# A two-layer vision block on one core: evacuations, norm statistics and the order of the stages changed

## The chip, the cores and the metric

The kernel runs on one core of a Trainium2 chip. The metric is the device time of one execution in microseconds (us). The core has five engines with a program each: TensorE (PE; its weight loads are shown apart as PEld), VectorE (DVE), ScalarE (ACT), GpSimd (POOL) and SyncE (SP), which here only issues DMAs. They meet through semaphores. Matrix products go to PSUM[...].

## The reference

The input is 32 images of 56 x 56 tokens with 96 channels, float32. Two layers follow each other; each adds a mixer and a feed-forward network to the running value:

```python
x = x + attention(_ln_c(x))          # 7x7 windows, shifted by 3, 3 heads of 32, relative bias
t = t + ffn0(_ln_t(t))               # 96 -> 384 -> 96, operands rounded to fp8 (5,2), sums to (5,10)
x = x + ssm(_ln_c(x))                # norm again, expand to 2x192, gate, scan along the width, 192 -> 96
t = t + ffn1(_ln_t(t))

def _ln_c(v, eps=1e-6):
    m = jnp.mean(v, axis=-1, keepdims=True)
    s = jnp.var(v, axis=-1, keepdims=True)
    return (v - m) / jnp.sqrt(s + eps)
```

So there are four norms over the 96 channels of a token, called here "a" (attention), "f" (first network), "e" (state-space mixer, which the code folds into one norm) and "g" (second network). The scan of the mixer is written as a product with a 56 x 56 triangular matrix for each of 192 channels.

## The kernel before

The work is cut in 128 blocks of 14 image rows, held as a tile `xb` of 112 partitions (two window rows of 56 columns) by 7 x 96 values: 7 rows of tokens in each partition. Ten such tiles are in use in turn. A block is loaded, runs through all stages over several steps of the loop, is summed up in place and is stored from the same tile.

A norm has two stages. The first takes mean and variance of each of the 7 tokens of a partition, and GpSimd makes the power of -1/2; the second applies them:

```python
def ln_stats(i, name, scale, shift):
    xb = xtiles[i]
    st = one.tile([TP, G, 6], F32, tag=f"st_{name}", ...)
    mv = two.tile([TP, G, 2], F32, tag=f"mv_{name}", ...)
    for g in range(G):                                   # G = 7
        nc.vector.bn_stats(st[:, g, :], xb[:, g, :])
        nc.vector.bn_aggr(mv[:, g, :], st[:, g, :])
    rs = two.tile([TP, G], F32, tag=f"rs_{name}", ...)
    nc.vector.tensor_scalar(rs, mv[:, :, 1], scale, shift, op0=ALU.mult, op1=ALU.add)
    nc.gpsimd.tensor_tensor(rs, rs, neg_half, ALU.pow)
    state[name, i] = mv, rs

def ln_norm(i, name, dtype):
    ...
    for g in range(G):
        nc.vector.tensor_scalar(xn[:, g, :], xb[:, g, :], mv[:, g, 0:1], rs[:, g : g + 1],
                                op0=ALU.subtract, op1=ALU.mult, ...)
```

The products use PSUM tiles of two banks, four of them in turn. An output projection writes 4 tokens' columns to the first bank and 3 to the second, and each part is added to `xb` right after its own products:

```python
def out_banks(name):
    po = banks(name)                                     # [128, 2, 512], one of four
    ...                                                  # parts: (0, 4, bank 0), (4, 7, bank 1)

def att_out(i):                                          # tile "pr" in the profile
    xb = xtiles[i]
    for g0, g1, po in out_banks(f"pr_{i}"):
        for g in range(g0, g1):
            matmul(po[:, g - g0, :], ot[:, g]..., wo)
        add_to(xb, g0, g1, po)                           # VectorE

def ffn_out(i, layer):                                   # tiles "py_f", "py_g"
    for g0, g1, po in out_banks(f"py_{nm}"):
        for g in range(g0, g1):
            for hc in range(3):
                matmul(po[:, g - g0, :], hq[:, hc, ...], w2q[:, hc, :], ...)
        nc.scalar.copy(y16[:, g0:g1], po)
    nc.vector.tensor_tensor(y16, y16, b2q..., ALU.add)
    nc.gpsimd.tensor_tensor(xb, xb, y16, ALU.add)
```

`matmul` and `transpose` chain TensorE's instructions, so that they keep the order in which the stages are called; the other engines' instructions are put in an order by the framework. The loop calls the stages of different blocks in each step `t`; `run(lag, ...)` works on block `t - lag`, and `scan_some()` does one of the six scan units that each group of four blocks gives:

```python
for t in range(nblocks + 8):
    load(t + 2)
    run(0, att_tokens)              # tr_a
    run(7, ffn_tokens, 1)           # tr_g
    run(2, mix_tokens)              # tr_e
    run(0, att_qk)                  # qk
    run(7, ffn_hidden, 1)           # ph_g
    scan_some()
    run(1, ln_norm, "f", F8)
    run(0, att_v)                   # pv
    run(2, mix_expand, 0, 4)        # pu
    run(0, att_scores)              # sab, sc
    run(-1, ln_stats, "a", 1.0, LNC_EPS)
    run(7, ffn_out, 1)              # py_g
    run(7, store)
    run(2, mix_expand, 4, 7)        # pu
    if ...: scans += [...]          # every fourth step: six units
    run(1, ffn_tokens, 0)           # tr_f
    scan_some()
    run(6, mix_turn, 0, 4)          # gt
    run(0, att_values, nkeys)       # av
    scan_some()
    run(1, ffn_hidden, 0)           # ph_f
    run(6, mix_turn, 4, 7)          # gt
    scan_some()
    run(6, mix_out, 0)              # so
    run(0, att_back)                # tr_o
    run(6, mix_out, 1)              # so
    run(6, ln_stats, "g", 1.0, LNT_EPS)
    run(-1, ln_norm, "a", F32)
    scan_some()
    run(1, ffn_out, 0)              # py_f
    run(1, stats_e)
    run(0, att_out)                 # pr
    run(6, ln_norm, "g", F8)
    run(0, ln_stats, "f", 1.0, LNT_EPS)
    run(1, ln_norm, "e", F32)
    scan_some()
```

Of the kernel before, what the change touches and what calls it, by code (L numbers as in the profile page):

```python
# [23 lines left out]
C = 96  # L24
# [11 lines left out]
TP = 2 * HW  # L36
G = 7
# [6 lines left out]
HALF = NPAIR * W2  # L44
MASKED = -1.0e30
LNC_EPS = 1e-6
LNT_EPS = 1e-5
# [7 lines left out]
def kernel(  # L55
# [27 lines left out]
    nc = tc.nc  # L83
    nimg = x.shape[0]
    nblocks = nimg * NBLK
# [3 lines left out]
    one = ctx.enter_context(tc.tile_pool(name="one", bufs=1))  # L89
    two = ctx.enter_context(tc.tile_pool(name="two", bufs=2))  # L90
# [6 lines left out]
    def queued(ins):  # L97

        if last[0] is not None:
            tc.add_manual_dep(ins.ins, last[0], order, reason="order of the stages")  # L100
        last[0] = ins.ins.name

    def matmul(*args, start=True, stop=True):
        queued(nc.tensor.matmul(*args, start=start, stop=stop))  # L104
# [4 lines left out]
    def banks(name):  # L109

        return psum.tile([128, 2, 512], F32, tag="ps", name=name)
# [14 lines left out]
    xtiles = {}  # L126

    def load(i):
        if i >= nblocks:
            return  # L130
        xb = xpool.tile([TP, G, C], F32, tag="xb", name=f"xb_{i}")
        for dst, src in block_dmas(i, x, xb):
            nc.sync.dma_start(dst, src)
        xtiles[i] = xb
# [73 lines left out]
    wso = weights([2, C], F32, "wso")  # L208
# [85 lines left out]
    for w in range(HW):  # L294
        eng = nc.scalar if w % 2 else nc.sync
# [44 lines left out]
    xws, vs, gTs, xqs = [], [], [], []  # L340
    for n in range(2):
# [4 lines left out]
        gT = const.tile([128, 4 - n, 2, TP], F32, name=f"gT_{n}")  # L346
# [19 lines left out]

    def ln_stats(i, name, scale, shift):

        xb = xtiles[i]
        st = one.tile([TP, G, 6], F32, tag=f"st_{name}", name=f"st_{name}{i}")  # L370
        mv = two.tile([TP, G, 2], F32, tag=f"mv_{name}", name=f"mv_{name}{i}")
        for g in range(G):
            nc.vector.bn_stats(st[:, g, :], xb[:, g, :])  # L373
            nc.vector.bn_aggr(mv[:, g, :], st[:, g, :])
        rs = two.tile([TP, G], F32, tag=f"rs_{name}", name=f"rs_{name}{i}")
        nc.vector.tensor_scalar(rs, mv[:, :, 1], scale, shift, op0=ALU.mult, op1=ALU.add)
        nc.gpsimd.tensor_tensor(rs, rs, neg_half, ALU.pow)  # L377
        state[name, i] = mv, rs

    def ln_norm(i, name, dtype):  # L380
        xb = xtiles[i]
        mv, rs = state.pop((name, i))
        saturate = {"saturate": False} if dtype == F8 else {}
        xn = one.tile([TP, G, C], dtype, tag=f"xn_{name}", name=f"xn_{name}{i}")
        for g in range(G):
            nc.vector.tensor_scalar(  # L386
                xn[:, g, :],
                xb[:, g, :],
                mv[:, g, 0:1],
                rs[:, g : g + 1],  # L390
                op0=ALU.subtract,
                op1=ALU.mult,
                **saturate,
            )
        state["n" + name, i] = xn

# [13 lines left out]
    def out_banks(name):  # L410

        po = banks(name)
        parts = []
        for n, (g0, g1) in enumerate(((0, 4), (4, 7))):
            parts.append((g0, g1, po[0:TP, n, 0 : (g1 - g0) * C].rearrange("p (g c) -> p g c", c=C)))
        return parts

    def add_to(xb, g0, g1, po):
        nc.vector.tensor_tensor(xb[:, g0:g1, :], po, xb[:, g0:g1, :], ALU.add)  # L419

    state = {}
# [8 lines left out]
    def att_qk(i):  # L430
        xw = xws[i % 2]
        for n, dst in ((0, qT), (1, kT)):
            pq = banks(f"qk_{i}_{n}")
            for half in range(2):
                matmul(
                    pq[0:C, half, 0:HALF],
                    wqkv[:, n * C : (n + 1) * C],
                    xw[:, half * HALF : (half + 1) * HALF],
                )
            dst2 = dst[:, 0:NTOK].rearrange("c (h t) -> c h t", h=2)  # L440
            if n == 0:
                nc.scalar.copy(dst2, pq[0:C, :, 0:HALF])
            else:
                nc.vector.tensor_copy(dst2, pq[0:C, :, 0:HALF])

    def att_v(i):
        xw = xws[i % 2]
# [124 lines left out]
    def ffn_out(i, layer):  # L572
        w2q, b2q = ffns[layer][2:4]
        xb = xtiles[i]
        hq = state.pop(("hq", layer, i))
        nm = f"{'fg'[layer]}{i}"
        y16 = one.tile([TP, G, C], F16, tag="y16", name=f"y16_{nm}")
        for g0, g1, po in out_banks(f"py_{nm}"):
            for g in range(g0, g1):
                for hc in range(3):  # L580
                    matmul(
                        po[:, g - g0, :],
                        hq[:, hc, g * TP : (g + 1) * TP],
                        w2q[:, hc, :],
                        start=(hc == 0),
                        stop=(hc == 2),
                    )
            nc.scalar.copy(y16[:, g0:g1], po)  # L588
        nc.vector.tensor_tensor(y16, y16, b2q[:, None, :].to_broadcast([TP, G, C]), ALU.add)
        nc.gpsimd.tensor_tensor(xb, xb, y16, ALU.add)  # L590
# [65 lines left out]
            pt[0:C].rearrange("c b (s w) -> c (b s) w", w=RS)[:, 0 : 4 * n, 0:HW],  # L656
        )

    def mix_out(i, part):
        if part == 0:  # L660
            state["so", i] = out_banks(f"so_{i}")
        g0, g1, po = state["so", i][part]
        gT = gTs[part]
        for g in range(g0, g1):
            for eh in range(2):
                matmul(po[:, g - g0, :], gT[:, g - g0, eh, :], wso[:, eh, :], start=(eh == 0), stop=(eh == 1))
        add_to(xtiles[i], g0, g1, po)


    def pipeline(att_scores, nkeys):  # L670
        last[0] = None
        scans = []
        load(0)
        load(1)

        def stats_e(i):

            ln_stats(i, "e", 1.0 + SSM_EPS, SSM_EPS * LNC_EPS)

        def scan_some():  # L680
            if scans:
                scan_unit(*scans.pop(0))

        ln_stats(0, "a", 1.0, LNC_EPS)
        ln_norm(0, "a", F32)
        for t in range(nblocks + 8):
            load(t + 2)

            def run(lag, stage, *args):
                if 0 <= t - lag < nblocks:  # L690
                    stage(t - lag, *args)

            run(0, att_tokens)
            run(7, ffn_tokens, 1)
            run(2, mix_tokens)
            run(0, att_qk)
            run(7, ffn_hidden, 1)
            scan_some()
            run(1, ln_norm, "f", F8)
            run(0, att_v)  # L700
            run(2, mix_expand, 0, 4)
            run(0, att_scores)
            run(-1, ln_stats, "a", 1.0, LNC_EPS)
            run(7, ffn_out, 1)
            run(7, store)
# [3 lines left out]
            run(1, ffn_tokens, 0)  # L709
            scan_some()  # L710
            run(6, mix_turn, 0, 4)
            run(0, att_values, nkeys)
            scan_some()
            run(1, ffn_hidden, 0)
            run(6, mix_turn, 4, 7)
            scan_some()
            run(6, mix_out, 0)
            run(0, att_back)
            run(6, mix_out, 1)
            run(6, ln_stats, "g", 1.0, LNT_EPS)  # L720
            run(-1, ln_norm, "a", F32)
            scan_some()
            run(1, ffn_out, 0)
            run(1, stats_e)
            run(0, att_out)
            run(6, ln_norm, "g", F8)
            run(0, ln_stats, "f", 1.0, LNT_EPS)
# [59 lines left out]
```

## Time and profile before

The time is 6432.64 us (median of 3 runs, 6429.61 to 6435.65); the profiled execution spans 6430.6 us.

| | busy us | share | instructions |
|---|---|---|---|
| TensorE products | 4698.8 | 73% | 76574 |
| TensorE weight loads | 3807.1 | 59% | 76574 |
| VectorE | 3914.0 | 61% | 15036 |
| ScalarE | 2183.7 | 34% | 3841 |
| GpSimd | 1505.8 | 23% | 1227 |

In lists of the profile a group is named by line, engine, operation and the tiles it writes and reads, as `pr<-wo,ot`; products all have the line of their helper, so they are told apart by tiles. `st_a`, `mv_a`, `rs_a` and `xn_a` are the statistics, the aggregates, the factors and the normed tile of norm "a", and so on for the others. What stands in brackets behind an instruction is how long its engine had been idle, and whose signal ended that. An engine that is idle while another holds the end back costs nothing; TensorE's waits are read with that in mind.

The first `tr_a` starts 262 us into the span, after the preparation of the weights and of the scan's matrix; the last one ends at 6212.7.

### The profile page before, as it was taken

To read this page: it belongs to the slowest core of one execution; us is meant where nothing else is said; L and a number is where in the kernel's file an instruction comes from. 1 tells how busy PE (TensorE), PEld (TensorE's weight loads), DVE (VectorE), ACT (ScalarE), POOL (GpSimd) and SP (SyncE) were. 2 spreads that over 40 slices of the span, in tenths; PEclk is the share of its full clock that TensorE was granted. 3 is DMA by queue.
4 is the path that set the end of the run, shared out by engine and by line. 5 is a ranking of instruction groups with operands and counts; after the bars stand their busy time and mean duration, and the time that the engine had idled before them with its cause. 6 is when DMAs were issued, how large, how long until landed. Compare 5 with 4: busy or idle time off the path is not lost. (4 is left out here: it accounts for less than half of the span.)

```text
span 6430.6 us, 177667 instructions
## 1 busy us (share of the span) xinstructions
PE 4698.8 (73%) x76574; PEld 3807.1 (59%) x76574; DVE 3914.0 (61%) x15036; ACT 2183.7 (34%) x3841; POOL 1505.8 (23%) x1227
## 2 busy tenths in 40 slices
PE   0287877777777777777777787777787777787785
PEld 0166666665656666666666566666566666665664
DVE  1166666666666666665666666666666666666663
ACT  0033333333333333333333333333343333333342
POOL 1022222222222222222222222222222222222221
PEclk9888887887878888878888888888787888887886
DMA  2200000000000000000000000000000000000000
GB/s 17 32 10 13 14 14 15 13 15 15 15 14 14 14 14 14 16 14 14 15 15 13 16 13 14 15 14 15 15 15 14 14 14 15 15 15 14 13 12 15
DMA packets 232549, 94.56 MB, mean 15 GB/s; under 512 B 231214, under 2 KB 231696, under 8 KB 231696
## 3 DMA queue, kind: packets, MB, share of 16 engines
q1 hardware_dynamic: 215620, 80.79, 5.3%
q10 hardware_dynamic: 16132, 2.31, 0.7%
q8 instruction: 602, 9.86, 0.6%
q14 instruction: 195, 1.60, 0.1%
HBM read 42.05 MB, written 38.62 MB: 13 GB/s over the span
## 5 line engine op out<-in xcount | busy, mean ns | idle before, releaser
L104 PE MATMUL pu<-weg,xs 128*128 128x288 f32 (+1 forms) x3584 | 815.5, 387 | 0.5 <-issue 0.5
L104 PEld LDWEIGHTS pu<-weg,xs 128*128 128x128 f32 x3584 | 651.8, 219 | 142.4 <-issue 0.4
L104 PE MATMUL pr<-wo,ot 128*112 128x96 f32 x1792 | 270.1, 299 | 585.0 <-DVE xb L419 583.9
L373 DVE BATCH_NORM_STATS2 st_a<-xb 112x6 f32<-112x96 f32 x896 | 196.2, 233 | 799.6 <-DMA xb<-in_x_dram 797.4
L104 PEld LDWEIGHTS pr<-wo,ot 128*112 128x112 f32 x1792 | 227.9, 202 | 607.1 <-DVE xb L419 605.6
L104 PE MATMUL qk<-xw,wqkv 128*96 128x392 f32 x1024 | 571.5, 726 | 3.3 <-ACT xw L428 3.3
L104 PE MATMUL scan<-u,toep 64*64 64x28 f32 x24576 | 459.3, 231 | 34.6 <-issue 16.2
L104 PE MATMUL py_g<-w2q,hq_g 128*112 128x96 fp8e5 x2688 | 227.1, 244 | 343.8 <-DVE u L615 210.6
L104 PEld LDWEIGHTS scan<-u,toep 64*64 64x64 f32 x24576 | 433.5, 149 | 70.7 <-issue 33.3
L428 ACT COPY xw<-tr_a 96x448 f32<-96x448 f32 (+1 forms) x256 | 116.6, 510 | 1021.4 <-PE tr_a L107 1009.7
L386 DVE TENSOR_SCALAR xn_g<-xb,mv_g,rs_g 112x96 fp8e5<-112x96 f32 x896 | 331.4, 412 | 205.9 <-POOL rs_g L377 205.9
L104 PE MATMUL so<-wso,gT 128*112 128x96 f32 x3584 | 403.6, 265 | 32.3 <-DVE xb L419 29.7
L564 ACT CAST h_f<-ph_f 128x784 f16<-128x784 f32 x384 | 287.2, 820 | 400.4 <-PE ph_f L104 400.4
L615 DVE COPY u<-pu 128x384 f32<-128x384 f32 (+1 forms) x512 | 256.3, 502 | 269.1 <-ACT gt L614 266.4
L104 PEld LDWEIGHTS <-hq_g 128*112 128x112 fp8e5 x2688 | 205.5, 160 | 361.0 <-issue 288.6
L104 PEld LDWEIGHTS so<-wso,gT 128*112 128x112 f32 x3584 | 375.2, 179 | 58.7 <-issue 53.0
L567 POOL CAST hq_f<-h_f 128x784 fp8e5<-128x784 f16 x128 | 134.0, 1047 | 1146.4 <-DVE h_f L565 1146.4
L104 PEld LDWEIGHTS qk<-xw,wqkv 128*96 128x96 f32 x1024 | 247.7, 254 | 255.1 <-issue 250.4
L614 ACT ACTIVATE gt<-pu 128x384 f32<-128x384 f32 (+1 forms) x512 | 231.0, 451 | 492.9 <-PE pu L104 490.9
L104 PE MATMUL av<-v,pT 64*64 64x33 f32 x12288 | 388.6, 221 | 6.6 <-ACT pT L481 5.8
L104 PEld LDWEIGHTS av<-v,pT 64*64 64x64 f32 x12288 | 373.4, 136 | 30.1 <-issue 23.0
L567 POOL CAST hq_g<-h_g 128x784 fp8e5<-128x784 f16 x128 | 137.5, 1074 | 944.9 <-DVE h_g L565 509.3
(139 smaller groups left out, 10206.8 us busy)
## 6 DMA issues: line engine op xcount, KB each, us to landing
xb<-in_x_dram SPq DMA_DIRECT2D x224, 139.1 KB
out_dram<-xb SPq DMA_DIRECT2D x224, 139.1 KB
xb<-in_x_dram SPq DMA_DIRECT2D x224, 7.9 KB
out_dram<-xb SPq DMA_DIRECT2D x224, 7.9 KB
xb<-in_x_dram SPq DMA_DIRECT2D x32, 79.5 KB
out_dram<-xb SPq DMA_DIRECT2D x32, 79.5 KB
toep<-toep SPq DMA_DIRECT2D x1, 2352.0 KB
xb<-in_x_dram SPq DMA_DIRECT2D x32, 59.6 KB
```

The source lines that it names most:

```text
L104: queued(nc.tensor.matmul(*args, start=start, stop=stop))
L373: nc.vector.bn_stats(st[:, g, :], xb[:, g, :])
L386: nc.vector.tensor_scalar(xn[:, g, :], xb[:, g, :], mv[:, g, 0:1], rs[:, g : g + 1], op0=ALU.subtract, op1=ALU.mult, **saturate,)
L428: nc.scalar.copy(order[:, g0:g1], pt.rearrange("c (a w b) -> c a w b", a=g1 - g0, b=WS))
L564: nc.scalar.copy(h16[:, hc].rearrange("p (h t) -> p h t", h=2), ph[:, :, 0:HALF])
L567: nc.gpsimd.tensor_copy(hq[:, hc], h16[:, hc], saturate=False)
L614: nc.scalar.activation(gt[:, rp : rp + n, :], pu[:, 0:n, 0:E], AF.Tanh, scale=0.5)
L615: nc.vector.tensor_copy(u[:, rp : rp + n, :], pu[:, 0:n, E : 2 * E])
```

## The change

It has five parts. Statistics are taken of two tokens by one instruction: `bn_stats` gives count, mean and count times variance of the elements at even and at odd places apart, so two tokens are read interleaved, and no aggregate is needed; the seventh token is read twice. Norm "a" is applied by GpSimd. Both copies of q and k out of PSUM are ScalarE's. The output projections write both banks before either is evacuated. And the stages are called in a new order, meant to put enough other work of TensorE between a stage and the one that uses its result; the last lags grow by one, and a block's tile is loaded anew right after its store.

```diff
 def ln_stats(i, name, scale, shift):
-        st = one.tile([TP, G, 6], F32, tag=f"st_{name}", name=f"st_{name}{i}")
-        mv = two.tile([TP, G, 2], F32, tag=f"mv_{name}", name=f"mv_{name}{i}")
-        for g in range(G):
-            nc.vector.bn_stats(st[:, g, :], xb[:, g, :])
-            nc.vector.bn_aggr(mv[:, g, :], st[:, g, :])
+        st = two.tile([TP, G + 1, 3], F32, tag=f"st_{name}", name=f"st_{name}{i}")
+        for g in range(0, G, 2):
+            pair = xb[:, g : g + 2, :] if g + 1 < G else xb[:, g : g + 1, :].to_broadcast([TP, 2, C])
+            nc.vector.bn_stats(st[:, g : g + 2, :].rearrange("p g s -> p (g s)"), pair.rearrange("p g c -> p c g"))
+        mean, var = st[:, 0:G, 1], st[:, 0:G, 2]
-        nc.vector.tensor_scalar(rs, mv[:, :, 1], scale, shift, op0=ALU.mult, op1=ALU.add)
+        nc.vector.tensor_scalar(rs, var, scale / C, shift, op0=ALU.mult, op1=ALU.add)
 ...
 def ln_norm(i, name, dtype):
+        eng = nc.gpsimd if name == "a" else nc.vector
-            nc.vector.tensor_scalar(
+            eng.tensor_scalar(
 ...
 def att_qk(i):
-            if n == 0:
-                nc.scalar.copy(dst2, pq[0:C, :, 0:HALF])
-            else:
-                nc.vector.tensor_copy(dst2, pq[0:C, :, 0:HALF])
+            nc.scalar.copy(dst2, pq[0:C, :, 0:HALF])
 ...
 def att_out(i):
-        for g0, g1, po in out_banks(f"pr_{i}"):
+        parts = out_banks(f"pr_{i}")
+        for g0, g1, po in parts:
             for g in range(g0, g1):
                 matmul(po[:, g - g0, :], ot[:, g].rearrange("c w b -> c (w b)"), wo)
+        for g0, g1, po in parts:
             add_to(xb, g0, g1, po)
 ...                                  # ffn_out likewise; mix_out(i) does both parts, then both adds
-        for t in range(nblocks + 8):
-            load(t + 2)
+        for t in range(nblocks + 9):
```

The loop's body in the new order:

```python
run(0, att_tokens)              # tr_a
run(8, ffn_out, 1)              # py_g
run(8, store)
load(t + 2)
scan_some()
run(0, att_qk)                  # qk
run(1, ln_norm, "f", F8)
scan_some()
run(7, mix_turn, 0, 4)          # gt
run(0, att_v)                   # pv
scan_some()
run(1, ffn_tokens, 0)           # tr_f
run(7, mix_turn, 4, 7)          # gt
run(0, att_scores)              # sab, sc
run(-1, ln_stats, "a", 1.0, LNC_EPS)
run(-1, ln_norm, "a", F32)
scan_some()
run(1, ffn_hidden, 0)           # ph_f
run(7, mix_out)                 # so
run(7, ln_stats, "g", 1.0, LNT_EPS)
scan_some()
run(0, att_values, nkeys)       # av
run(2, mix_tokens)              # tr_e
run(1, ffn_out, 0)              # py_f
run(0, att_back)                # tr_o
run(7, ln_norm, "g", F8)
run(2, mix_expand, 0, 4)        # pu
run(1, stats_e)
run(0, att_out)                 # pr
run(0, ln_stats, "f", 1.0, LNT_EPS)
run(7, ffn_tokens, 1)           # tr_g
run(2, mix_expand, 4, 7)        # pu
if ...: scans += [...]          # every fourth step: six units
run(7, ffn_hidden, 1)           # ph_g
run(1, ln_norm, "e", F32)
scan_some()
```

More of the change, by code (lines that the diff above doesn't have):

```diff
@@ L369, in ln_stats @@
         xb = xtiles[i]
-        st = one.tile([TP, G, 6], F32, tag=f"st_{name}", name=f"st_{name}{i}")
-        mv = two.tile([TP, G, 2], F32, tag=f"mv_{name}", name=f"mv_{name}{i}")
-        for g in range(G):
-            nc.vector.bn_stats(st[:, g, :], xb[:, g, :])
-            nc.vector.bn_aggr(mv[:, g, :], st[:, g, :])
+        st = two.tile([TP, G + 1, 3], F32, tag=f"st_{name}", name=f"st_{name}{i}")
[3 more added lines that the diff above has]
+        mean, var = st[:, 0:G, 1], st[:, 0:G, 2]
         rs = two.tile([TP, G], F32, tag=f"rs_{name}", name=f"rs_{name}{i}")
-        nc.vector.tensor_scalar(rs, mv[:, :, 1], scale, shift, op0=ALU.mult, op1=ALU.add)
+        nc.vector.tensor_scalar(rs, var, scale / C, shift, op0=ALU.mult, op1=ALU.add)
         nc.gpsimd.tensor_tensor(rs, rs, neg_half, ALU.pow)
-        state[name, i] = mv, rs
+        state[name, i] = mean, rs
     def ln_norm(i, name, dtype):
         xb = xtiles[i]
-        mv, rs = state.pop((name, i))
+        mean, rs = state.pop((name, i))
+        xn = one.tile([TP, G, C], dtype, tag=f"xn_{name}", name=f"xn_{name}{i}")
+        eng = nc.gpsimd if name == "a" else nc.vector
         saturate = {"saturate": False} if dtype == F8 else {}
-        xn = one.tile([TP, G, C], dtype, tag=f"xn_{name}", name=f"xn_{name}{i}")
         for g in range(G):
[L386 to L393, printed above, removed]
+            col = slice(g, g + 1)
+            eng.tensor_scalar(
+                xn[:, g, :], xb[:, g, :], mean[:, col], rs[:, col], op0=ALU.subtract, op1=ALU.mult, **saturate
             )
@@ L577, in ffn_out @@
         y16 = one.tile([TP, G, C], F16, tag="y16", name=f"y16_{nm}")
-        for g0, g1, po in out_banks(f"py_{nm}"):
+        parts = out_banks(f"py_{nm}")
+        for g0, g1, po in parts:
             for g in range(g0, g1):
@@ L587, in ffn_out @@
                     )
+        for g0, g1, po in parts:
             nc.scalar.copy(y16[:, g0:g1], po)
@@ L657, in mix_turn, with mix_out @@
         )
[L659 to L667, printed above, removed]
+    def mix_out(i):
+        parts = out_banks(f"so_{i}")
+        for gT, (g0, g1, po) in zip(gTs, parts):
+            for g in range(g0, g1):
+                for eh in range(2):
+                    matmul(po[:, g - g0, :], gT[:, g - g0, eh, :], wso[:, eh, :], start=(eh == 0), stop=(eh == 1))
+        for g0, g1, po in parts:
+            add_to(xtiles[i], g0, g1, po)
     def pipeline(att_scores, nkeys):
@@ L693, in pipeline @@
             run(0, att_tokens)
-            run(7, ffn_tokens, 1)
-            run(2, mix_tokens)
+            run(8, ffn_out, 1)
+            run(8, store)
+            load(t + 2)
+            scan_some()
             run(0, att_qk)
-            run(7, ffn_hidden, 1)
+            run(1, ln_norm, "f", F8)
             scan_some()
-            run(1, ln_norm, "f", F8)
+            run(7, mix_turn, 0, 4)
             run(0, att_v)
-            run(2, mix_expand, 0, 4)
+            scan_some()
+            run(1, ffn_tokens, 0)
+            run(7, mix_turn, 4, 7)
             run(0, att_scores)
             run(-1, ln_stats, "a", 1.0, LNC_EPS)
-            run(7, ffn_out, 1)
-            run(7, store)
+            run(-1, ln_norm, "a", F32)
+            scan_some()
+            run(1, ffn_hidden, 0)
+            run(7, mix_out)
+            run(7, ln_stats, "g", 1.0, LNT_EPS)
+            scan_some()
+            run(0, att_values, nkeys)
+            run(2, mix_tokens)
+            run(1, ffn_out, 0)
+            run(0, att_back)
+            run(7, ln_norm, "g", F8)
+            run(2, mix_expand, 0, 4)
+            run(1, stats_e)
+            run(0, att_out)
+            run(0, ln_stats, "f", 1.0, LNT_EPS)
+            run(7, ffn_tokens, 1)
             run(2, mix_expand, 4, 7)
@@ L708, in pipeline @@
                 scans += [((t - 2) // NBLK, e0) for e0 in range(0, EH, UNIT)]
[L709 to L727, printed above, removed]
+            run(7, ffn_hidden, 1)
             run(1, ln_norm, "e", F32)
```

## The prediction

> **What bounds the kernel now.** I read the page's totals first, then the list of waits, then the order of time of the sync queue (SP) and of one whole step, and last the clock of short stretches. The kernel runs 128 blocks through one software pipeline, one step for each block; TensorE (PE) takes its instructions in the order in which the program writes them.
>
> The page's first and second parts (busy time with share of the span and count; granted TensorE clock in 40 slices):
>
> ```profile
> PE 4698.8 (73%) x76574; PEld 3807.1 (59%) x76574; DVE 3914.0 (61%) x15036; ACT 2183.7 (34%) x3841; POOL 1505.8 (23%) x1227
> PEclk9888887887878888878888888888787888887886
> ```
>
> No engine is full, and PE works at a granted clock of 0.82. A loop with PE at 73% is a loop of waits. The longest ones that matter, from the list of waits (who waited for whom: us in total, times, longest):
>
> ```profile
> DVE st_a L373 <- DMA xb<-in_x_dram: 797.4, 99, 174.9
> ...
> PE pr L104 <- DVE xb L419: 583.9, 128, 14.3
> ```
>
> VectorE waits for an input load at the statistics of norm "a" (797.4 less 174.9 at the start leaves 622 us), and PE waits at the second bank of the attention's output projection `pr` (584 us). They are partly the same time, as one heavy step shows in order of time (start, duration, engine and line; in brackets the idle time before and what ended it):
>
> ```profile
> 3109.94 0.99 PE L104 MATMUL pr<-wo,ot 128*112 128x96 f32 x8
> ...
> 3111.36 0.80 DVE L386 TENSOR_SCALAR xn_g<-xb,mv_g,rs_g 112x96 fp8e5<-112x96 f32 x3
> 3123.58 0.42 DVE L373 BATCH_NORM_STATS2 st_a<-xb 112x6 f32<-112x96 f32 x2 [11.43 <-DMA xb<-in_x_dram]
> 3123.92 0.49 DVE L589 TENSOR_TENSOR y_f<-y_f,b2q 112x672 f16<-112x672 f16 x1
> 3124.32 0.55 DVE L419 TENSOR_TENSOR xb<-pr,xb 112x384 f32<-112x384 f32 x1
> ...
> 3124.93 1.44 PE L104 MATMUL pr<-wo,ot 128*112 128x96 f32 x6 [13.99 <-DVE xb L419]
> ```
>
> The first bank of `pr` is done at 3110.9. Its evacuation stands on VectorE behind a statistic whose block hasn't landed, and PE's second bank, in the program behind that evacuation, waits 14 us. The statistic needn't stand there: its block is used a step and more later; VectorE's order in the trace runs ahead of the written one. The load is late because its buffer is that of the block stored last (10 buffers, all in use):
>
> ```profile
> 3089.08 14.90 SPq L138 DMA_DIRECT2D out_dram<-xb  x4
> 3107.21 13.57 SPq L133 DMA_DIRECT2D xb<-in_x_dram  x4
> ```
>
> From store to usable block: 3089.1 to 3123.6, 34.5 us; in a light step 3003.5 to 3037.8, 34.3 us. Store to store in light steps is 44.1 us (3003.5 to 3047.6), so a loop is closed: store, load, statistic, the VectorE work behind it, `py_g`, sum, store: 34.3 + 9.8. The steps show it too. Their starts (first `tr_a`) in one cycle of four lie at 2975.6, 3021.2, 3065.4, 3129.9, 3166.1, so 45.6, 44.2, 64.5 and 36.2 us, 190.5 in all, and the cycle repeats within 1 us. The step of 64.5 is the one with most of the scan; the one of 36.2 follows the long stall, where the load is early.
>
> The last view is the clock (columns: stretch, us, busy of PE, PEld, DVE, ACT and POOL, then PEclk, DMA share, GB/s):
>
> ```profile
> 3034.00:3042.00 8.00, 6.10 (x149) 5.25 (x148) 5.09 (x22) 3.65 (x6) 1.12 (x1) 1.00 0.05 12
> ...
> 3125.00:3129.00 4.00, 4.00 (x109) 3.83 (x110) 3.20 (x27) 0.00 (x0) 1.55 (x2) 0.50 0.01 4
> ```
>
> After the stall PE goes on at half clock: the second bank's six `pr` take 1.44 us there, against 0.83 at 3020.56 in the timeline of a light step.
>
> **What the Trainium skill says.** "TensorE: Matmul & The Clock Gate", Part 1, has the array fall to half its clock after an idle window of about 3.4 us and return after a busy one. The trace agrees in kind: 0.50 after the 14 us stall. "Perfetto Trace Analysis", Optimizing Tensor Performance, wants independent groups to rotate through banks so that the evacuation of one overlaps the matmuls of the next; the projections of the kernel before don't, though their two parts lie in two banks. "SBUF — State Buffer", Who interferes with whom, says that GpSimd and a VectorE instruction with two SBUF inputs or in a two-port mode lock each other out for a whole instruction; the trace doesn't separate this. "GPSIMD Engine Reference", 3.1, has about 2.6 cycles per element for two inputs; the addition of 672 elements here took 1461 ns, 2.2 ns an element.
>
> **The change, part by part,** for a cycle of four steps (190.5 us) unless said.
>
> Floor of PE. At full clock the stages of one step, read off the same timeline, take: tr_a 0.7, qk 2.6 (half of the 5.1 at half clock), pv 1.5, scores 1.25, av 2.9, tr_o 1.0, pr 1.65; tr_f 0.35, ph_f 1.2, py_f 1.2; tr_e 0.85, pu 3.0 + 2.2, gt 1.7, so 2.8; tr_g 0.35, ph_g 1.2, py_g 1.25: 27.7 us. Six scan units of 2.0 make 12 more, once a cycle. Floor: 4 x 27.7 + 12 = 123 us.
>
> Both banks ahead. `pr`: 583.9 / 128 = 4.6 us a step is removed as a direct wait; `py_g` (1.0) and `py_f` (0.6) between their banks; `so` 0.25. Sum 6.4 us a step, 26 a cycle. But of `pr`'s wait only the ordinary 2.0 us is the bank order's own; the rest of the heavy step's 14 us is the DMA's, and moves on unless the load comes in time. So 4 x (2.0 + 1.0 + 0.6 + 0.25) = 15 us are certain, and half-clock work goes with it.
>
> Statistics. Seven pairs of stats and aggregate at 0.225 us a pair (starts 3126.39, 3126.62, 3126.84 in the heavy step) are 1.6 us. Four instructions of 192 elements: two in a row of 96 took 0.42, so 0.19 each, plus 96 elements at 1.0 ns (392 elements took 558 ns, 448 took 614), 0.29 each, 1.15 us. Saved 0.43 x 16 = 7 us of VectorE, nothing if the strided read costs double.
>
> Norm "a" to GpSimd: 260.3 / 128 = 2.0 us a step off VectorE, 8 a cycle. On GpSimd a small operation took 248 ns (96x32 product) and a copy of 392 elements 529, so an estimate of 0.3 to 0.4 us, 7 of them 2.1 to 2.8 us, on an engine that is busy 46 of 190. kT's copy: 0.97 us a step from VectorE to ScalarE (0.81 there), 4 a cycle. VectorE falls from 120.9 to about 102 a cycle, ScalarE rises from 68 to 71. Neither is the bound then.
>
> The order. It puts most consumers well behind their producers: so to tr_g 11.8 us of PE work, pr to tr_f 14, tr_e to pu only 2.2, against 1.3 us on ScalarE and 0.5 on GpSimd. One place is worse: hidden layer 1 (`ph_g`) ends a step and its use `py_g` comes after tr_a alone. At the tail, ph_g to py_g took 4.6 us; ph_g and tr_a cover 2.0. That is a new wait of about 2.6 us in three steps of four, where no scan lies between.
>
> The loop of the DMA. Store and load now start together, some 8 us into step t (tr_a, wait, py_g, evacuation 0.9, sum 0.5, GpSimd 1.5), so a block is usable at 8 + 34.3 = 42 us, and its statistic is written in step t+1. Written there it would wait for nothing. If VectorE's order again runs ahead, it does. In the kernel before, the statistic stood some 20 us of undisturbed PE work behind the store (y_g's sum at 3089 to the second bank of py_f at 3110), a mismatch of 14 us to the real 34.3. In the new order VectorE has little room there (about 13 us of work in the last 15 of a step), and room at the start of the next step, 24 to 26 us behind the store; the mismatch is then about 9 us.
>
> Sum. Light: 27.7 + 2.6 + about 1 of bank waits = 31, plus 9 minus some slack: 39.5. The light step with a scan unit in it: 41.5. Heavy, five units: 31 + 10 = 41, plus 11 for an earlier place of the statistic: 52. Cycle 2 x 39.5 + 41.5 + 52 = 172.5 against 190.5. The loop from first to last `tr_a` takes 5950 us now (262 to 6212): 5950 x 172.5/190.5 = 5390. Start 262, tail 218 plus about 20 for one more step of lag. Sum 5890; as the two ends below are unequal, I put the middle at 5800.
>
> **Rivals.** (1) The DMA loop stays whole: mismatch 14 and the new py_g wait. Light 46, heavy 58, cycle 196, time 6600; for it speaks that each light step before is exactly such a loop, against it that store and load are issued earlier relative to the next store and that VectorE has 19 us a cycle less to do. (2) The loop is cut: the order hides the load. Then the cycle is 123 plus 4 x 3.5 to 6 of waits, with a fuller clock, 140 to 150, time 4900 to 5200; the 36.2 us step of the kernel before, where no load was waited for and which still had 2.0 + 0.8 + 0.6 us of bank waits, speaks for it. (3) GpSimd becomes the wait: seven norms ahead of a power of 1.5 us delay xn_g or xn_f by 3 us; the transposes have 10 us of slack, so this alone adds little. If one norm took 1 us, 7 a step, some 3 us a step come on top: about 6200.
>
> **Range and chances.** Rival 1 and a slow GpSimd get 0.2 together, rival 2 0.15, the middle the rest. 5300 to 6250 should hold it; faster by over 2% (below 6304) 0.80, within 0.10, slower 0.10.
>
> **What would show it.** Right: pr's wait for xb gone from the list; step starts 39 to 42 apart with one near 52; st_a still waiting for its DMA, some 5 us a step; a few us before py_g for hq_g; mean clock about 0.85; norm "a" at 0.3 to 0.4 us each on GpSimd. Wrong: no wait for the load at all (then 5000), or one of over 10 us in each step (then 6400 and more); norms of 1 us; statistics of over 0.4 us each.

## The result, and the profile after

| | before | after |
|---|---|---|
| time, us (median; lowest to highest) | 6432.74 (6429.61 to 6435.65) | 6202.85 (6199.58 to 6211.59) |
| mean granted TensorE clock | 0.824 | 0.849 |
| mean cycle of four steps, us | 191.1 | 184.3 |
| last `tr_a` to the end, us | 218 | 218 |

After / before is 0.9645, 95% interval 0.9628 to 0.9662. The change gains 230 us where 630 were forecast: the direction is right, and the time lies near the upper end of the range.

The first and second parts of the page of the kernel after (busy time, share of the span, count; granted clock in 40 slices):

```profile
PE 4452.3 (72%) x76574; PEld 3653.7 (59%) x76574; DVE 3248.8 (52%) x8892; ACT 2271.3 (37%) x3969; POOL 2177.4 (35%) x2123
PEclk9988888888888888888888888888888788888896
```

VectorE has lost 665 us of work (3914.0 before), and TensorE is as far from full as it was. Between the profiled spans (6430.6 and 6200.5 us) lie 230 us. TensorE's busy time for the same 76574 products fell by 246 us (4698.8 to 4452.3), at a clock of 0.849 for 0.824; its idle time rose, from 1732 us to 1748. So the whole gain is that the same products run faster; the waits were moved, not taken away. From the list of waits of the kernel after (who waited for whom: us in total, times, longest):

```profile
DVE st_a L376 <- DMA xb<-in_x_dram: 1364.7, 123, 177.1
...
PE pu L104 <- DVE u L615: 532.6, 91, 16.0
...
PE py_g L104 <- POOL hq_g L565: 266.2, 98, 6.4
```

`pr`'s wait of 584 us for `xb` is gone. The statistic's wait for its load has nearly doubled (without the one at the start, 1188 us for 622), and a new wait of TensorE, `pu` for `u`, of up to 16 us stands in the list (and one of `py_f` for `xb`, 227.9 us in all, up to 11.1). They are the old one at another place. VectorE in one step of the kernel after, in order of time (start, duration; in brackets the idle time before and what ended it):

```profile
3168.94 0.36 DVE L376 BATCH_NORM_STATS2 st_a<-xb 112x6 f32<-112x192 f32 x1 [16.26 <-DMA xb<-in_x_dram]
...
3169.69 0.55 DVE L615 COPY u<-pu 128x384 f32<-128x384 f32 x1
```

and TensorE there:

```profile
3170.29 1.70 PE L104 MATMUL pu<-weg,xs 128*128 128x288 f32 x4 [15.98 <-DVE u L615]
```

The statistic stands ahead of `u<-pu`, the evacuation that TensorE needs, and waits for a transfer. TensorE waits 16 us behind it for a copy that itself takes half a us. The steps start at 3050.5, 3090.3, 3124.4, 3175.8 and 3234.5, so they last 39.8, 34.1, 51.4 and 58.7 us. The two long ones hold a stall of VectorE of 15 to 16 us each: this one, and one that ends at 3215.5, ahead of `xb<-so`. The other two statistics of the cycle wait 2.7 and 5.7 us, ahead of `y_g`, early in the steps that start at 3090.3 and 3124.4.

The loop through the memory has a chain of its own now. From the chain that ended last, kernel after (start, duration, what; "SPq" is the sync queue issuing descriptors):

```profile
3063.46 0.24 SPq L138
...
3075.36 6.25 DMA out_dram<-xb
...
3082.32 5.60 SPq L133
...
3088.28 9.40 DMA xb<-in_x_dram
...
3097.81 0.89 DVE st_a L376 x3
3098.70 0.42 DVE y_g L589
...
3099.18 1.48 POOL xb L590
...
3100.67 0.24 SPq L138
```

Store, load, statistic, `y_g`, sum, next store: the loop of the kernel before, closed again, here 37.2 us long. And on the chain just ahead of this piece stands GpSimd's norm:

```profile
3051.47 6.07 POOL xn_a L391 x7
3057.53 0.80 POOL hq_g L565
```

Seven norms of 0.87 us on average delay the cast `hq_g`, that delays `py_g`, and the store starts 13 us into its step, not 8 (10, 13 and 5.5 us in the three steps behind it).

### The profile page after: what moved, and what is told of

It is laid out like the page before. It is cut to its first block, busy times and chain, and to the rows that moved or that the text cites. A ratio compares the mean times of both kernels' runs of the same rounds, so it can differ in the third digit from the quotient of the medians.

```text
span 6200.5 us, 172319 instructions
## 1 busy us (share of the span) xinstructions
PE 4452.3 (72%) x76574; PEld 3653.7 (59%) x76574; DVE 3248.8 (52%) x8892; ACT 2271.3 (37%) x3969; POOL 2177.4 (35%) x2123
## 4 chain that ended last, share of the span: by engine, by line
DMA 33%; SPq 24%; PE 16%; DVE 13%; POOL 9%; issue 3%; ACT 1%; DVEq 0%; ACTq 0%; POOLq 0%
DMA xb<-in_x_dram 16%; DMA out_dram<-xb 15%; SPq L133 13%; SPq L138 11%; POOL xn_a L391 3%; POOL xb L590 2%; DMA toep<-taps_d 2%; PE scan L104 2%; PE qk L104 2%; PE py_g L104 2%; DVE xn_g L391 2%; PE av L104 1%; POOL rs_g L380 1%; PE so L104 1%; PE pu L104 1%
## 5 line engine op out<-in xcount | busy, mean ns | idle before, releaser
L376 DVE BATCH_NORM_STATS2 st_a<-xb 112x6 f32<-112x192 f32 x512 | 163.1, 352 | 1372.8 <-DMA xb<-in_x_dram 1364.7
L391 POOL TENSOR_SCALAR xn_a<-xb,st_a,rs_a 112x96 f32<-112x96 f32 x896 | 696.5, 792 | 28.0 <-PE tr_a L107 13.4
L380 POOL TENSOR_TENSOR rs_f<-rs_f,neg_half 112x7 f32<-112x7 f32 x128 | 205.0, 1602 | 873.0 <-DVE rs_f L379 873.0
L104 PE MATMUL qk<-xw,wqkv 128*96 128x392 f32 x1024 | 504.7, 652 | 8.4 <-ACT xw L427 8.3
L104 PE MATMUL py_g<-w2q,hq_g 128*112 128x96 fp8e5 x2688 | 255.6, 256 | 343.4 <-POOL hq_g L565 266.2
L590 POOL TENSOR_TENSOR xb<-xb,y_g 112x672 f32<-112x672 f32 x128 | 186.9, 1460 | 745.8 <-DVE y_g L589 745.8
L380 POOL TENSOR_TENSOR rs_g<-rs_g,neg_half 112x7 f32<-112x7 f32 x128 | 192.3, 1502 | 722.7 <-DVE rs_g L379 721.7
L391 DVE TENSOR_SCALAR xn_g<-xb,st_g,rs_g 112x96 fp8e5<-112x96 f32 x896 | 362.5, 459 | 102.2 <-POOL rs_g L380 102.2
L595 ACT ACTIVATE xs<-tr_e,bet,gam 96x448 f32<-96x448 f32 (+1 forms) x256 | 158.9, 669 | 680.7 <-PE tr_e L107 657.3
L632 DVE SCALAR_TENSOR_TENSOR gt<-gt,scan 128x448 f32<-128x448 f32 x384 | 219.8, 613 | 316.7 <-PE scan L104 316.7
L104 PE MATMUL py_f<-w2q,hq_f 128*112 128x96 fp8e5 x2688 | 195.1, 235 | 249.2 <-DVE xb L418 227.9
```

What stands on the lines that cost most here:

```text
L376: nc.vector.bn_stats(st[:, g : g + 2, :].rearrange("p g s -> p (g s)"), pair.rearrange("p g c -> p c g"))
L391: eng.tensor_scalar(xn[:, g, :], xb[:, g, :], mean[:, col], rs[:, col], op0=ALU.subtract, op1=ALU.mult, **saturate)
L595: nc.scalar.activation(xs[0:C, g0:g1, 0:2, 0:HW], pt.rearrange("c (g r w) -> c g r w", r=2, w=HW), AF.Identity, bias=bet, scale=gam,)
L632: nc.vector.scalar_tensor_tensor(part, part, 1.0, py[:, eh, 0 : UNIT * NRP].rearrange("p (e q) -> p q e", q=NRP), op0=ALU.add, op1=ALU.mult,)
```

## The experiments

The theory: VectorE's order runs ahead of the written one, and a statistic that stands ahead of its load holds up evacuations; the other parts of the change work, but what they free is handed to this wait. The rivals: the store and load are too slow for ten tiles, wherever the statistic stands; or a new wait (GpSimd's norm, the order) has eaten the gain. "Open loop" below is a kernel in which the statistic may run ahead, "held" one in which it may not.

**1 and 2. The statistic held, in the kernel after and in the kernel before.** An ordering edge (both ends are on VectorE; nothing new is waited for on another engine) puts the statistic of norm "a" behind the last evacuation of the scores, where it is written.

```diff
 def att_scores(i): ...
+        ev = nc.vector.scalar_tensor_tensor(pa, ps, QSCALE, bt, ...)   # last evacuation
+    held[0] = ev.ins.name
 def ln_stats(i, name, scale, shift): ...
+            ins = nc.vector.bn_stats(...)
+            if name == "a" and held[0] is not None:
+                tc.add_manual_dep(ins.ins, held[0], order, ...)        # order alone, no semaphore
```

> The changed kernel with one edge more: on VectorE the statistics of norm a must stand behind the last evacuation of the scores that are written before them in the program, so they are never moved ahead to a place where their block has not landed. Nothing is computed otherwise. Theory (the loop store, load, statistic, store through VectorE's order sets the step): the wait of st_a for its load falls from 1365 us to under 250 (177 of it at the start), pu's wait for u and py_f's for xb go with it, the cycle of four steps falls from 184 to about 145 us and the time to 4950 to 5200. Rival (GpSimd's norm and PSUM evacuation set the step, the DMA wait is where idle VectorE happens to sit): the time stays within 2% of 6203.

> The kernel before with the same edge alone. Theory: its loop of 34.3 + 9.8 us is cut as well; what is left are the waits between the two banks (2.0 + 1.0 + 0.6 + 0.25 us a step) and the transposes' waits; a step is like the 36 us one that met no late load, the heavy one 46 to 48: cycle about 155, time 5200 to 5450. Then the order of the stages and the banks are worth 3 to 6% once the loop is gone. Rival (the bank order is the cause of the heavy step's 14 us wait): still 6300 or more, with a long wait of pr for xb.

Measured: after held 5530.8 us, 0.8596 of before (0.8582 to 0.861), cycle 161.2; before held 5634.6, 0.8761 (0.8746 to 0.8775), cycle 164.2. In both, the load's wait is the one at the start alone. From the list of waits of the kernel after, held:

```profile
DVE st_a L376 <- DMA xb<-in_x_dram: 174.6, 1, 174.6
```

and the shares of the chain that ended last, by engine, of the kernel after and then of the kernel after, held:

```profile
DMA 33%; SPq 24%; PE 16%; DVE 13%; POOL 9%; issue 3%; ACT 1%; DVEq 0%; ACTq 0%; POOLq 0%
```

```profile
DVE 28%; issue 25%; POOL 24%; PE 20%; ACT 3%; DMA 0%; SPq 0%; POOLq 0%; DVEq 0%; ACTq 0%
```

DMA and its queue were 57% of the chain and are 0%, with the same tiles and transfers. The slow-transfer rival is out. The edge alone takes 672 us off the kernel after and 798 off the kernel before: about three times what the change as a whole brought. Neither got as far as expected; what bounds them next is in experiments 6 to 9 and 11.

**3. An eleventh tile.** More slack for the load; it is written at the head of the step, so that the extra tile can be used.

```diff
-    xpool = ctx.enter_context(tc.tile_pool(name="xpool", bufs=10))
+    xpool = ctx.enter_context(tc.tile_pool(name="xpool", bufs=11))
+            load(t + 2)                # first in the step
             run(0, att_tokens)
             run(8, ffn_out, 1)
             run(8, store)
-            load(t + 2)
```

> The changed kernel with 11 block tiles in place of 10 and the load called first in a step, so that a load never waits for the store of the same step; VectorE's order is left to the framework. Theory: load to usable block is 16 to 17 us and starts with the step, no store ahead of it; the statistic can be moved ahead of it by some us only: st_a's wait 250 to 600 us, time 5050 to 5500. Rival: within 2% of 6203.

Measured: 6400.5 us, 0.9949 of before (0.9932 to 0.9965): 3.2% slower than the kernel after. The expectation fell. From its list of waits, and its sync queue in order of time:

```profile
DVE st_a L376 <- DMA xb<-in_x_dram: 1186.7, 122, 175.0
```

```profile
3045.16 14.92 SPq L138 DMA_DIRECT2D out_dram<-xb  x4
3063.36 13.29 SPq L133 DMA_DIRECT2D xb<-in_x_dram  x4
```

The load still follows a store by 18 us, only for a block one further on, and VectorE still waits over 1000 us for it. The statistic was moved ahead by the same block: among 90 blocks in the middle of the run, the kernel after has 45 statistics one block ahead of `tr_a`, as written, and 45 two blocks ahead; with the eleventh tile 45 stand two and 45 three blocks ahead. Why `py_g`'s wait for `hq_g` doubled, to 567.1 us, wasn't looked into, and the tile and the place of the load weren't tried apart.

**4. Norm "a" back on VectorE**, all else as after.

```diff
-        eng = nc.gpsimd if name == "a" else nc.vector
+        eng = nc.vector
```

> The changed kernel with norm a back on VectorE. GpSimd needs 792 ns for each of its seven instructions, 5.5 us a block, and the cast of hq_g stands behind it there; py_g waited 266 us for that cast. Theory that this is inside the loop of the DMA: 2 us a step less, 5950 to 6100. Theory that the loop hides it: 6203 within 1%. If it is slower by over 1%, freeing VectorE was worth more than GpSimd's delay costs.

Measured: 6093.5 us, 0.9469 of before (0.9454 to 0.9485). Norm "a" on GpSimd costs 109 us here. Its group in the kernel after, with one more fact in it (busy, mean ns | idle time before):

```profile
L391 POOL TENSOR_SCALAR xn_a<-xb,st_a,rs_a 112x96 f32<-112x96 f32 x896 | 696.5, 792 | 28.0 <-PE tr_a L107 13.4
```

792 ns on average (median 694, up to 1906), where VectorE in the kernel before took 336 (busy 260.3 us for 896, overlaps counted once), and I had estimated 300 to 400 for GpSimd.

**5. The banks alone**, on the kernel before.

```diff
-        for g0, g1, po in out_banks(f"pr_{i}"):
+        parts = out_banks(f"pr_{i}")
+        for g0, g1, po in parts:
             for g in range(g0, g1):
                 matmul(po[:, g - g0, :], ...)
+        for g0, g1, po in parts:
             add_to(xb, g0, g1, po)     # ffn_out likewise
```

> The kernel before with both banks of pr and of py written ahead of their evacuation, nothing else. Theory (the loop of the DMA sets the step, and the banks' waits lie inside its slack or move): pr's wait for xb goes from 584 us to nearly nothing and the time stays within 2% of 6433. Rival (the waits add up): 6.1 us a step less, 5650 to 5800.

Measured: 6381.75 us, 0.9912 (0.9896 to 0.9929). From its list of waits:

```profile
PE tr_e L107 <- DVE mv_f L374: 586.7, 127, 15.9
PE tr_g L104 <- DVE xn_g L386: 388.6, 192, 3.6
```

`pr` no longer waits for `xb`, but in the stages that follow it `tr_e` waits 587 us where it waited 150 before, and `tr_g` 389 where it waited 153. 51 us are left of the gain.

**6. The banks alone, held.** Experiments 2 and 5 together.

> The same with the edge that keeps the statistics of norm a behind the scores. Theory: with the loop cut the banks' waits are on the path: 2.0 + 1.0 + 0.6 us a step and the half clock behind them, 250 to 500 us under the held kernel of before (5635), so 5130 to 5390. Rival (the steps are set by VectorE or by other waits): within 1.5% of 5635.

Measured: 5605.8 us, 0.871 (0.8695 to 0.8724), 29 us less than experiment 2. The expectation fell: without any wait for the load, too, `pr`'s 246.5 us are replaced, by `tr_g` (387.6, from 68.5) and `tr_e` (277.0, from 152.3). In the old order these stages come close behind `pr` and want the same VectorE.

**7. The kernel after, held, with norm "a" on VectorE** (1 and 4 together).

> The changed kernel with the edge and with norm a on VectorE. In the held changed kernel GpSimd spends 5.1 us a block on the norm, the cast of hq_f waits behind it and py_f waits 2.7 us for that cast in three steps of four. Theory: those 264 us go, and half-clock stretches with them: 5100 to 5300, the fastest so far. Rival (VectorE needs the room): 5500 or more.

Measured: 5370.2 us, 0.8342 (0.8324 to 0.8361), cycle 156.5, and 70 us over the range that was expected. GpSimd's norm costs 161 us where the loop is cut.

**8. As 7, with the old statistics.**

```diff
-        for g in range(0, G, 2):
-            pair = ...
-            nc.vector.bn_stats(st[:, g : g + 2, :]..., pair...)
-        mean, var = st[:, 0:G, 1], st[:, 0:G, 2]
+        for g in range(G):
+            nc.vector.bn_stats(st[:, g, :], xb[:, g, :])
+            nc.vector.bn_aggr(mv[:, g, :], st[:, g, :])
+        mean, var = mv[:, :, 0], mv[:, :, 1]
```

> The previous kernel with the statistics as before: seven instructions and seven aggregates a norm. The interleaved pairs took 0.28 us each (four in 1.15), 1.15 a norm against 1.6: 1.8 us a step of VectorE. If VectorE is on the path of a held step: 100 to 230 us slower than the kernel with the interleaved statistics; if it isn't: the same within 1%.

Measured: 5539.7 us, 0.8609 (0.8591 to 0.8628). The interleaved statistics are worth 170 us there.

**9. As 7, with each bank evacuated before the next** (`pr`, `py_f` and `py_g` as in the kernel before: the diff of experiment 5 the other way round; `so` stays as it is).

> The held changed kernel with norm a on VectorE, and each bank of pr and py evacuated before the next one is written, as in the kernel before (so stays as changed). In the old order the banks were worth 29 us with the loop cut, because tr_g and tr_e, next on TensorE, waited for VectorE instead (388 + 277 us). In the new order other work stands behind pr and py. Theory that banks and order are worth something only together: 200 to 450 us slower than 5370. Rival (banks are worth little anywhere): within 1% of 5370.

Measured: 5900.1 us, 0.9175 (0.9158 to 0.9193), cycle 172.7; `pr` waits 341.1 us for `xb` again. In the new order the banks are worth 530 us, more than was expected, in the old one 29. The new order without them is slower than the old order held (5634.6). The two parts work only together: the banks take away a wait, and the order sees to it that there is other work to do in its stead.

**10. Order, banks and kT's copy without the rest**: the kernel after, open loop, with norm "a" on VectorE (as in 4) and the old statistics (as in 8).

> The changed kernel without the edge, with norm a on VectorE and with the statistics as before: of the change, the order, the banks and the copy of k are left. Theory (the loop of the DMA hides most of what the parts do): between 6093 (with the new statistics) and 6433, about 6200 to 6300. If the order and the banks are what the change gained in the open loop: 6100 to 6200; if the statistics are: 6300 to 6430.

Measured: 6629.97 us, 1.0306 of before (1.0289 to 1.0323): slower, which none of the three expectations had. From 3075.7 on, steps of 45.2, 46.8, 59.2 and 46.8 us. Its list of waits:

```profile
DVE st_a L376 <- DMA xb<-in_x_dram: 1521.9, 123, 174.3
...
PE ph_g L104 <- DVE xb L419: 930.2, 89, 12.5
```

and VectorE in one of its steps:

```profile
3071.95 0.26 DVE L376 BATCH_NORM_STATS2 st_a<-xb 112x6 f32<-112x96 f32 x1 [12.01 <-DMA xb<-in_x_dram]
...
3072.19 0.91 DVE L419 TENSOR_TENSOR xb<-pr,xb 112x384 f32<-112x384 f32 x2
```

The statistic stands ahead of both evacuations of `pr`; now that both banks are written, both wait together, and `ph_g` behind them. So the 230 us add up, in the order in which they were put together, as +197 (order, banks, copy), -537 (statistics; 6630.0 to 6093.5) and +109 (norm on GpSimd). Held, the same three steps are -95 (5634.6 to 5539.7), -170 and +161.

**11 and 12. A better order.** In experiment 7 TensorE loses its clock most of all in one place: of 960 us at half clock after the first 600 us of the run, 519 lie where `py_g` has the longest of the waits around the fall. From the order of time of its TensorE, and the clock of one stretch (stretch, us, busy of PE, PEld, DVE, ACT and POOL, PEclk, DMA share, GB/s):

```profile
3030.41 0.25 PE L104 MATMUL py_g<-w2q,hq_g 128*112 128x96 fp8e5 x1 [0.63 <-ACT xw L430]
3031.77 0.33 PE L104 MATMUL py_g<-w2q,hq_g 128*112 128x96 fp8e5 x1 [1.11 <-POOL hq_g L569]
3032.31 2.01 PE L104 MATMUL py_g<-w2q,hq_g 128*112 128x96 fp8e5 x19 [0.21 <-DVE hq_g L571]
3034.12 4.59 PE L104 MATMUL qk<-xw,wqkv 128*96 128x392 f32 x8
```

```profile
3033.00:3039.00 6.00, 6.00 (x28) 3.61 (x27) 1.20 (x4) 1.84 (x4) 1.46 (x1) 0.61 0.05 13
```

The list of waits charges `py_g` with 1.95 us here, but the half clock that follows (0.61 in this stretch) costs another 1.7 in `qk` (4.59 us against 2.87 at full clock) and 0.8 in `py_g` itself (2.01 for 19 products; 1.32 for all 21 at full clock in experiment 12). Experiment 11 puts `py_g`, with the store and the load, behind `qk`, and the first part of `gt` and a scan unit ahead of it; experiment 12 also parts `tr_o` and `pr` from what they wait for:

```diff
             run(0, att_tokens)              # tr_a
+            run(7, mix_turn, 0, 4)          # gt, from behind qk
+            scan_some()
+            run(0, att_qk)
             run(8, ffn_out, 1)              # py_g
             run(8, store)
             load(t + 2)
 ...                                         # experiment 12 only:
             run(1, ffn_out, 0)
-            run(0, att_back)                # tr_o
             run(7, ln_norm, "g", F8)
             run(2, mix_expand, 0, 4)
+            run(0, att_back)
+            run(7, ffn_tokens, 1)
             run(1, stats_e)
+            run(2, mix_expand, 4, 7)
             run(0, att_out)                 # pr
             run(0, ln_stats, "f", 1.0, LNT_EPS)
-            run(7, ffn_tokens, 1)
-            run(2, mix_expand, 4, 7)
```

> The held changed kernel with norm a on VectorE, with py_g called behind qk in place of ahead of it, and the first gt ahead of qk. In the kernel without this move py_g waits some 1.9 us a step for hq_g and leaves itself and part of qk at half clock, about 2.5 us more. Expected if these waits are on the path: 3 to 4 us in three of four steps, 5000 to 5150. If VectorE sets the step instead: within 1.5% of 5370.

> As late_py, and tr_o called behind the first half of the expansion (it waits 1.5 us a step for an), pr behind the second half. Expected: 1 us a step less than late_py, 4900 to 5050; if the waits only move to pu or tr_g: as late_py within 1%.

Measured: 4970.5 us, 0.7723 (0.771 to 0.7736), and 4924.8 (4914.8 to 4932.9), 0.7656 (0.7641 to 0.7671); cycles 144.0 and 141.7. The first move alone is worth 400 us, and the mean clock goes from 0.903 to 0.951. `py_g`'s waits for GpSimd and VectorE were 178 us in experiment 7 (108.5 and 69.4), and 9 are left. Of the 390 us between the two profiled spans, TensorE's idle time makes 123; the other 267 are its busy time for the same 76574 products (4436.1 to 4169.5), so the clock is the larger part. The parts of the first move weren't tried one by one. Experiment 12 leaves nothing of the computation out and is the fastest kernel here, 21% below the kernel after. The first part of its page, and a store, a load and the next store in its sync queue:

```profile
PE 4226.9 (86%) x76574; PEld 3501.9 (71%) x76574; DVE 3402.0 (69%) x9788; ACT 2260.5 (46%) x3969; POOL 1579.7 (32%) x1227
```

```profile
3022.51 15.07 SPq L138 DMA_DIRECT2D out_dram<-xb  x6
3040.79 13.47 SPq L133 DMA_DIRECT2D xb<-in_x_dram  x4
3054.30 15.52 SPq L138 DMA_DIRECT2D out_dram<-xb  x4
```

TensorE is at 86%. The next store is issued 0.04 us after the load's issue ends, and so it is with two of the four stores of a cycle: the queue, with 32 us a block, is now about as long as a light step (31 to 34 us). That it is their floor wasn't tested. The statistic waits for its load again, 82 us in all beside the 176 at the start. Loads and stores on two queues are what I would try next; it wasn't tried.

## Why the prediction was off, step by step

- **What bounds the kernel:** right. With the statistic held, either kernel is 11 to 12% faster and the load's wait is gone (experiments 1 and 2).
- **The sum: this is the step that failed.** It counts TensorE's stages at full clock, 123 us a cycle, and adds 49.5 us in which TensorE waits: 36.5 for the loop of the DMA (8.5 in each light step, 11 in the heavy one) and 13 for the rest. In the mean of 22 cycles of the kernel after, TensorE is busy for 137.8 us and idle for 46.6. The waits of the sum are thus nearly right; what it leaves out is the 15 us by which the products take longer at half clock, although it expected a mean clock of about 0.85, which came (0.849). The cycle is 184.3 us for 172.5, 12 us or some 370 us over 31 cycles; the sum of 5890 was then moved by 90 to a middle of 5800, and the tail gave back 20. Held, where no statistic waits after the start, TensorE is busy for 137.7 us all the same, so cutting the loop doesn't bring these 15 us back. The first move of experiment 11, which takes `py_g`'s short waits away, brings 9 of them (137.2 to 128.2). No run has the loop closed and the clock full, so what these 15 us would have brought by themselves is not shown.
- **The waits of the sum** are right by luck: held, TensorE is idle for 23.3 us a cycle where the sum has 13 without the loop, and the loop adds 23.3 where it has 36.5.
- **The loop of the DMA:** the mechanism is right, and so is the total that the statistic waits: 2.7, 5.7, 16.3 and 14.9 us, 39.6 a cycle, for the 9, 9, 9 and 11 of the prediction (the "some 5 us a step" among its signs was too low). Its place is wrong. I reasoned that VectorE would have room for the statistic only at the start of the next step. Two of four do stand early in the step after their store; the other two stand in the very step of their store (stores at 3137.6 and 3181.3, statistics at 3168.9 and 3215.5). So the steps last 39.8, 34.1, 51.4 and 58.7, not 39.5, 39.5, 41.5 and 52. Why the framework's order puts them there was not measured. What was: with slower statistics all of the 90 blocks in the middle of the run have theirs two blocks ahead (experiment 10), and holding it leaves all 90 one block ahead.
- **Both banks ahead:** 15 us a cycle were called "certain". Alone they gave 51 us, under 2 a cycle, in the open loop, and 29 held; with the new order, held, 530, or 17 a cycle (experiments 5, 6, 9). The estimate was right only for the pair; a wait taken away where the next stage wants the same engine is not removed but passed on.
- **Statistics:** each was to take 0.29 us, four 1.15. Four in a row take 1.14 to 1.15 (0.35 alone, but the next starts 0.28 on). Their effect was thought 7 us a cycle; it is 170 us held (some 5 a cycle) but 537 in the open loop (17 a cycle), since there they also change where the load's wait falls.
- **Norm "a" on GpSimd:** estimated 0.3 to 0.4 us each, measured 0.79: 5 to 6 us a block, ahead of `hq_g` or `hq_f`. It costs 109 to 161 us. Rival 3 named this and nearly its size per norm (1 us), not its route: it reaches TensorE by the casts queued behind it. That rival's time of about 6200 is the one measured by luck, since it had 3 us a step, some 370 us in all, for the norms.
- **The order:** `py_g`'s new wait of 2.6 us came as 2.7 (266.2 / 98), partly for another reason: without the norm on GpSimd it is 1.1 (108.5 / 98 in experiment 7). I left out what such a wait does to the clock, and that was the larger part (experiment 11).
- **Tail:** +20 us was expected, 218 us it stayed.
- **Rivals:** the first, the loop whole, 46 and 58 a step and 6600 us, is what order and banks did by themselves (45 to 47 and 59; 6630). The second, the loop cut, a cycle of 140 to 150 and 4900 to 5200 us, is experiments 11 and 12: it needs the edge, the norm back on VectorE and `py_g` moved, none of which the change has.

## What to carry to other kernels

When an engine that works in order waits for a transfer, ask first whether the waiting instruction had to stand there, and hold it back by an ordering edge, before adding buffers or cutting work: here the edge brought 672 to 798 us and an eleventh tile, with the load called earlier, made it slower. While such a loop is closed, the parts of a change can't be added up, for each is measured through where it moves that wait (537 us or 170 for the same statistics); cut the loop, then judge them. And price a wait of TensorE with the half clock that follows, not by its length alone: a sum of stages at full clock doesn't fit a kernel whose mean clock you expect to be 0.85.

## What was not expected of the hardware

**Short gaps cost the clock.** "TensorE: Matmul & The Clock Gate", Part 1, of the Trainium skill ties the fall to an idle window of about 3.4 us, and has frequent short idling between groups of products do it as well. Experiment 7 shows the second kind (stretch, us, busy of PE, PEld, DVE, ACT and POOL, PEclk, DMA share, GB/s):

```profile
3027.41:3030.82 3.41, 1.64 (x12) 0.90 (x9) 3.41 (x13) 3.12 (x5) 1.50 (x2) 1.00 0.07 20
3030.82:3034.24 3.42, 2.26 (x21) 2.10 (x22) 2.87 (x9) 0.00 (x0) 0.90 (x1) 0.50 0.08 22
3034.24:3037.65 3.41, 3.41 (x7) 1.56 (x7) 0.51 (x1) 1.38 (x3) 1.46 (x1) 0.50 0.04 11
```

TensorE was busy for 1.64 of 3.41 us, with no gap of over 0.98, and then ran at half clock for 6.8 us. Of the 184 falls of the clock after the first 600 us of this run, 94 have no gap of over 1.2 us in the 3.4 us before them.

**A VectorE instruction lasted until a GpSimd one ended.** The scale of the variances, `rs_a`, is 112 x 7 elements and took 171 ns on average before. In the kernel after, 90 of its 128 took over 400 ns, and all 90 ended within 40 ns of the end of a GpSimd instruction. VectorE and GpSimd in the kernel after:

```profile
3099.41 1.27 DVE L379 TENSOR_SCALAR rs_a<-st_a 112x7 f32<-112x7 f32 x1
```

```profile
3099.18 1.47 POOL L590 TENSOR_TENSOR xb<-xb,y_g 112x672 f32<-112x672 f32 x1 [6.09 <-DVE y_g L589]
```

One ends at 3100.68, the other at 3100.65. This fits "SBUF — State Buffer", Who interferes with whom, of the Trainium skill, by which an instruction of one of the two engines can hold the ports that they share to its end while the other is blocked. For a VectorE instruction with one input in SBUF the page has that in two-port modes alone, and whether `rs_a` ran in one the trace doesn't show. Held, `rs_a` takes 0.16 us again.

**Reading two rows alternately cost what was estimated.** Statistics of 192 elements, taken in turn from two rows, took 0.28 to 0.29 us each, four in a row; the estimate, from those of 96 elements and 1.0 ns for each further one, was 0.29. No statistic of 192 neighbouring elements was run.
